# Two stacked 5x5 convolutions: earlier additions to v, another buffer for one v, and column filtering in seven more chunks

## The chip, the cores and the metric

The kernel runs on one core of a Trainium2 chip. The metric is the device time of one execution in microseconds (us), lower is better. Five engines take their instructions in order from queues of their own: TensorE (PE: matrix products), VectorE (DVE: elementwise work), ScalarE (ACT: copies, scalings, activations with sums), GpSimd (POOL: small copies, and the issue of those DMAs that add to what is there) and SyncE (SP: the issue of other DMAs). They wait for one another by semaphores.

## The reference

The input x is 8 images of 32 channels, 252 x 252, in float32. Two layers of the same form follow each other:

```
def _gn(v, G=16, eps=1e-5):        # mean and variance over 2 channels and the image
    ...
    return ((g - m) / jnp.sqrt(s + eps)).reshape(v.shape)
x = x + _L0_conv_ref(_gn(x), L0_conv_weight)
x = x + _L1_conv_ref(_gn(x), L1_conv_weight)
```

`_L0_conv_ref` and `_L1_conv_ref` are 5 x 5 convolutions from 32 to 32 channels with reflected borders (written with FFTs). A layer can only begin on an image when that image's mean and variance are known; for the second layer these are those of the first layer's output.

## The kernel before

**Tiling.** The pixels of an image are put on the 128 partitions as 32 channels times 4 parities (even or odd row, even or odd column). A 5 x 5 filter becomes a 3 x 3 one on this grid. In the direction of rows the kernel uses a minimal filter with six points, numbered 0 to 5: from groups of rows it forms six combinations, multiplies each with transformed weights on TensorE, and puts four output rows together from the six products. An image of a layer is cut into 8 chunks; a chunk (b, l, c) is image b, layer l (0 or 1), chunk c. So there are 128 chunks. In a chunk each point takes three matrix products (one for each column of the filter) of 504 columns (layer 0) or 508 (layer 1). The trace shows each product as two records.

**Before the products**, in `transform`: `v` holds differences or sums of rows. In layer 0 VectorE forms it (`row_pairs`, L561). In layer 1 it is made by DMAs from GpSimd's queue (`row_sums`): L551 copies the chunk's rows of `y` (the first layer's output) into a `v` tile, and once the copy has landed L553 and L554 add further rows. Then VectorE forms from `v` and from the rows the operands: `point2` (L586), `point4` (L590), `point1` (L596), `point3` (L593), and for points 0 and 5 `points05` (L603). L590, L593 and L603 read `v`; L603 is its last reader.

**The v tiles.** There are two, with tags `va` and `v`, of one buffer each. Layer 0 uses `v`. Layer 1 uses `va`; only from chunk 6 of the last but one image on do layer-1 chunks take `va` and `v` in turn.

**Column filtering** (`by_columns`): in some chunks points 0 and 5 are not computed with 2 x 3 full products (group `sums`, written by L679), but with 8 products of half the width (L701), after a filter in the direction of columns as well. This asks for four more operations on VectorE ahead (`columns`: L612, L613 and L621, L622, or L616 in their place in layer 0), three behind (`column_parts`: L786, L787, L788) and one on ScalarE between the products (`seed_columns`: L705, which scales one PSUM bank into another). In layer 1 chunks 1, 3 and 5 do so, in the last image but one only 1 and 3.

**After the products**, in `conv`: ScalarE seeds the PSUM banks of points 1 and 3 (L723, L725) from those of points 2 and 4, and copies these to the tile `sd` (L731, L738). VectorE combines them (L742, L751, L752, L757, L758), ScalarE or VectorE writes the outer rows (L767, L779, L765), and in layer 1 ScalarE interleaves the output rows to `o` (L916), which SyncE stores. The products of points 0 and 5 of most chunks come one chunk late, behind the `m` and `pairs` products (points 2, 4 and 1, 3) of the next chunk.

**Statistics** (`finish_stats`): six small steps on VectorE, TensorE and ScalarE turn sums into mean and scale: `moments` (ends with L336), `group_mean` (TensorE, L342 and L344), `deviations` (begins with L351), `group_var` (L363), `variance` (L369, L371), `inverse` (L377 to L383). ScalarE scales the weights with the result (`scale_points`, L511, three pairs of points) and GpSimd adds the residual's own weights (`add_residual`, L479, four operations for each pair). For the last chunk of layer 0 of each image these steps run twice: for the next image's layer 0, and for this image's layer 1.

**Order.** All is put into one table with due times (`at`), sorted, and issued in that order (`manual_schedule`); on each engine the instructions keep it. A due time is thus only a place in a queue. `begin(i)` gives the planned start of the i-th chunk; it is shorter for chunks that filter by columns. Layer 0 of image b + 1 and layer 1 of image b take turns, chunk by chunk; two pairs are swapped, so that the sequence at the start of layer 1 is (1,0,0), (1,0,1), (0,1,0), (0,1,1), (1,0,2).

Of the kernel before, what the change touches and what calls it, by code (L numbers as in the profile page):

```python
# [56 lines left out]
def tile_conv_preact_x2(ctx: ExitStack, tc: tile.TileContext, x: bass.AP, w0: bass.AP, w1: bass.AP, out: bass.AP):  # L57
    nc = tc.nc
    B, C, H, W = x.shape
# [5 lines left out]
    NCH = 8  # L65
# [26 lines left out]
    def at(t: float, fn, *args, **kw):  # L92
        table.append((t, len(table), fn, args, kw))
# [67 lines left out]
    def once(b: int, c: int) -> bool:  # L161

        return c < (NCH - 1, 3)[b] if b < 2 else False

    def parts(b: int, c: int):

        if once(b, c):
            return ((0, 10), (10, 6)) if (b, c) == (0, 0) else ((0, 2), (2, 14))
        return ((0, ROWS),) + (((ROWS, 2),) if c == NCH - 1 else ())
# [216 lines left out]
    def finish_stats(b: int, l: int, *times):  # L386
        for t, fn in zip(times, (moments, group_mean, deviations, group_var, variance, inverse)):
            at(t, fn, b, l)
# [86 lines left out]
    def add_residual(eng, u, ks):  # L475
        for cp, rp in quads:
            to = (2 * (1 - cp) + (1 - rp)) * Q
            dst = u[quad(cp, rp), ks, 1 + cp, to : to + Q]
            eng.tensor_add(dst, dst, resid[quad(cp, rp), ks])  # L479
# [53 lines left out]
    def transform(t0: float, t1: float, b: int, l: int, c: int, free: float = -100.0, now=(0, 0, 0)):  # L533
# [4 lines left out]
        def source():  # L538
            if l == 0:
                nxt = xs[b, c + 1] if c + 1 < NCH else xtail[b]  # L540
                return xs[b, c][:, :, 0:256:2], nxt[:, :, 0:256:2]
            return ytile[b, c], ytile[b, c + 1] if c + 1 < NCH else ytail[b]

        def row_sums(add: bool):

            t, nxt = source()
            if not add:
                i = max(order.index((b, l, c)) - order.index((B - 2, 1, NCH - 2)), 0)
                got["v"] = vpool.tile([P, ROWS, wi], F32, tag=("va", "v")[i % 2], name=f"v_{b}_{l}_{c}")
                got["vt"] = got["v"].rearrange("p (t i) w -> p t i w", i=4)  # L550
                G.dma_start(got["v"], t)  # L551
            else:
                G.dma_start(got["v"][:, 0 : ROWS - 2], t[:, 2:ROWS], accum_op=ALU.add)  # L553
                G.dma_start(got["v"][:, ROWS - 2 : ROWS], nxt[:, 0:2], accum_op=ALU.add)  # L554
# [70 lines left out]
        if (b, l, c) == order[0]:  # L625
            at(t0 - 33.3, row_quads, 0, 2)
            at(t0 - 31, point2, 0, 2)
            for fn in (row_pairs, point4):
                at(t0, fn, 0, 2)
            at(t0 + 0.2, row_quads, 2, 4)  # L630
            at(t0 + 0.2, row_pairs, 2, 4)
            at(t0 + 0.2, last_rows)
            at(t0 + 0.2, point2, 2, 4)
            at(t0 + 0.2, point4, 2, 4)
            at(t0 + 4.9, point1)
            at(t0 + 5.5, point3)
            at(t0 + 6.2, points05)
        else:
            if l:
                two = begin(order.index((b, l, c)) - 2)  # L640
                at(two + 1.45, row_sums, False)
                at(two + 11.0, row_sums, True)
            else:
                at(t0, row_pairs)
            for dt, fn in ((2, row_quads), (3.2, last_rows), (3.6, point2)):
                at(t0 + dt, fn)
            at(max(t0 + 4.2, free + 9.45) if l else t0 + 4.2, point4)
            at(max(t0 + 5.5, free + 7.8), point1)
            at(max(t0 + 5.6, free + (11.1 if by_columns(*now) else 10.25)), point3)
            at(t1, points05)  # L650
            if by_columns(b, l, c):
                at(t1 + 1.5, columns)
# [292 lines left out]
    order = [(0, 0, c) for c in range(NCH)]  # L945
# [4 lines left out]
    for n in ((0, 1, 0), (B - 2, 1, NCH - 2)):  # L950
        i = order.index(n)
# [8 lines left out]
    def by_columns(b: int, l: int, c: int) -> bool:  # L960
        if l == 0:
            return c < NCH - 1 and (b > 1 or (b == 1 and c > 1))
        return c in ((1, 3, 5) if b == B - 1 else ((1, 3) if b == B - 2 else (1, 3, 5)))

    own = [5.1 if i in at_once else 1.7 if by_columns(*n) else 0.0 for i, n in enumerate(order)]
    late = [0.0 if i in at_once else 1.7 if by_columns(*n) else 5.1 for i, n in enumerate(order)]
# [1 line left out]
    def begin(i: int) -> float:  # L968

        return sum(10.2 + (own + [0.0])[j] + (late[j - 1] if j else 0.0) for j in range(i))  # L970


    t0 = -100.0
# [37 lines left out]
    at(t0 + 32.5, variance, 0, 0)  # L1011
    at(t0 + 33.5, inverse, 0, 0)
    transform(t0 + 64, 0.0, *order[0])
    at(t0 + 19, residual_blocks)
    at(t0 + 63.7, first_point, 2)
# [11 lines left out]
    for i, (b, l, c) in enumerate(order):  # L1027
        t0, t1, t2 = (begin(i + j) for j in range(3))
        if i in at_once:
            conv(b, l, c, t0, t1, m05=(extra[:, 0], extra[:, 1]))  # L1030
        elif i + 1 == len(order):

            conv(b, l, c, t0, t0 + 12.75, 0.0, 0, 2, m05=(extra[:, 0], extra[:, 1]))
            conv(b, l, c, t0 + 12.75, t0 + 20.4, 0.0, 2, 4, m05=(sums05[:, 0], sums05[:, 1]))
        elif i + 2 == len(order):
            conv(b, l, c, t0, t1, t1 + 10.3, later=5.1)
        else:
            conv(b, l, c, t0, t1, t2, later=10.2 + own[i + 1])
        if i + 1 < len(order):
            transform(t0 + (6.3 if i == 0 else 2.9), t1 + 0.2, *order[i + 1], free=t0, now=(b, l, c))  # L1040
            nb, nl, ncx = order[i + 1]
            k = inputs.index((nb, ncx)) + 2
            if nl == 0 and 2 < k < len(inputs):
                for part in parts(*inputs[k]):
                    early = once(*inputs[k]) or nb == 0
                    at(t0 + (14.0 if nb == 0 and part[0] == ROWS else 4.0 if early else 9.5), load, *inputs[k], *part)
                    at(t1 + (0.2 if early else 9.0), borders, *inputs[k], *part)
                    if once(*inputs[k]):
                        kb, kc = inputs[k]
                        t = 5.25 if part[0] == 0 and (kb, kc) != (1, 0) else 13.55 if kb else 8.5  # L1050
                        at(t1 + t, even_columns, *inputs[k], *part)
        if c == 0 and any(by_columns(b, l, k) for k in range(NCH)):
            t = begin(i - 1) if l == 0 and b > 1 else t2 if l == 0 else t0
            at(t + 5.4, halve_middle, b, l)
            at(t + 8.2, column_weights, b, l)
        if b and l == 0 and c == 0:
            at(t0 + 0.1, begin_sums, b, 1)

        if l == 0 and b + 1 < B:
            wide = 1 if b == 0 else 2  # L1060
            if c == 0:
                for j in range(2):
                    at(begin(i - 1) + 1.0 if b > 1 else t0 + (8.0 if b else 1.0), load_piece, b + 1, j)
            if c < NPIECE // 2:
                for j in range(2):
                    p = 2 * c + j
                    t = (t1 if wide == 2 and j else t0) + (8.6 + 2.5 * j if wide == 1 else 9.8)
                    if b == 1 and p < 4:
                        t = begin(NCH + (1, 1, 2, 2)[p]) + (9.8, 12.4, 9.8, 15.5)[p]
                    at(t, piece_sums, b + 1, p)  # L1070
                    if p + 2 < NPIECE:
                        at(t + 2.6, load_piece, b + 1, p + 2)
            if c == 2:
                at(t0 + 14, fetch_weights, b + 1, 0)
            if c == NCH - 1:
                finish_stats(b + 1, 0, *(t0 + t for t in (1.55, 3.5, 3.6, 6.9 if b else 7.7, 7.8, 8.4)))
                for j, ks in enumerate(pairs):
                    at(t0 + (9.5, 10.4, 11.3)[j], scale_points, b + 1, 0, ks)
                    at(t0 + (10.4, 12.3, 14)[j], lambda b=b, ks=ks: add_residual(G, scaled[b + 1, 0], ks))
        if l == 0 and c == NCH - 1:  # L1080
            te = t0 + 15.3
            at(te + 0.1, fetch_weights, b, 1)
            finish_stats(b, 1, *(te + t for t in (3.0 if b < B - 1 else 4.4, 6.85, 6.86, 10.25 if b else 9.9, 12.82, 13.55)))
            for j, ks in enumerate(pairs):
                at(te + (14.5, 15.5, 21)[j], scale_points, b, 1, ks)
                at(te + (15.5, 17.5, 22)[j], lambda b=b, ks=ks: add_residual(G, scaled[b, 1], ks))
# [36 lines left out]
```

## Time and profile before

| | us |
|---|---|
| median of 3 runs (range) | 1921.32 (1920.58 to 1922.4) |
| the profiled execution, whole | 1922.81 |
| its span, first to last instruction | 1921.0 |
| an image in the middle (377.87 to 608.12 and the like) | 229.7 to 230.3 |
| ScalarE busy, share of the span | 73% |
| DMA engines, mean busy share over a middle image | 0.94 to 0.95 |
| granted TensorE clock, mean | 0.99 |

In the lines of the profile "A <- B" tells which tile is written from which; a bracket at the end of a line in a timeline is the time that the engine was idle ahead of that instruction and what ended it. In the tables of waits the figures are total us, number, longest. A line of the table by stretches has the stretch, its length, then busy time and count for each of PE, PEld, DVE, ACT and POOL, and at the end the granted clock, the DMA share and GB/s. Durations of neighbouring instructions overlap a little, so that their distance from start to start is the better price of one in a row.

### The profile page before, as it was taken

The page shows a single profiled execution, that of the slowest core. Times are in us where ns is not written, and L with a number is a line of the kernel's source. Part 1 is how long each engine was busy: PE and PEld are TensorE (multiplying, and loading weights), DVE is VectorE, ACT ScalarE, POOL GpSimd, SP SyncE. Part 2 cuts the span into 40 slices and gives each one's busy share as a digit, 9 for nine tenths or more (in the row PEclk, how much of TensorE's full clock was granted, in tenths as well). Part 3 has the DMA queues.
Part 4 walks back from the last instruction along what each step waited for, and adds up shares of the span by engine and source line. Part 5 has one row for each costly group of instructions (what it writes and reads, how often), then busy time and mean ns, then how long its engine had stood idle before and what let it go on. Part 6 is the DMA issues. An engine that isn't in the chain of part 4 may idle for free.

```text
span 1921.0 us, 19939 instructions
## 1 busy us (share of the span) xinstructions
PE 1864.5 (97%) x5134; PEld 954.9 (50%) x5134; DVE 1673.9 (87%) x2923; ACT 1394.6 (73%) x2688; POOL 385.1 (20%) x733
## 2 busy tenths in 40 slices
PE   5998899999999999999999999999999999999998
PEld 4443355545555455544555445554455545544445
DVE  7987699989998899989999899997999989988675
ACT  5887577777787787777887777886787766665575
POOL 4542211131111211122111311113111131111210
PEclk8999899999999999999999999999999999999999
DMA  9877689989999899999999989998999978985695
GB/s 276 206 167 206 147 233 218 238 216 225 245 227 221 212 262 223 223 234 208 248 230 218 230 216 249 225 224 217 215 259 212 236 168 183 202 190 149 168 229 112
DMA packets 248626, 411.40 MB, mean 214 GB/s; under 512 B 19520, under 2 KB 215488, under 8 KB 238144
## 3 DMA queue, kind: packets, MB, share of 16 engines
q1 hardware_dynamic: 220384, 272.09, 60.4%
q0 software_dynamic: 27648, 135.28, 28.0%
q10 hardware_dynamic: 480, 2.77, 0.4%
q8 instruction: 40, 0.66, 0.1%
q14 instruction: 74, 0.61, 0.1%
HBM read 207.41 MB, written 67.39 MB: 143 GB/s over the span
## 4 chain that ended last, share of the span: by engine, by line
PE 83%; DMA 5%; ACT 4%; DVE 4%; issue 2%; POOL 1%; SPq 0%; ACTq 0%; DVEq 0%; POOLq 0%
PE pairs L679 30%; PE m L679 28%; PE sums L679 9%; PE extra L701 6%; PE sums L701 6%; PE extra L679 4%; DMA v<-y 2%; DMA st<-in_x_dram 2%; ACT o L916 1%; POOL u L479 1%; ACT junk L854 1%; ACT st L231 0%; ACT y L777 0%; ACT sd L731 0%; DVE sd L742 0%
## 5 line engine op out<-in xcount | busy, mean ns | idle before, releaser
L679 PE MATMUL m<-t,u 128*128 128x508 f32 (+3 forms) x1560 | 682.0, 585 | 21.4 <-POOL u L479 12.8
L679 PE MATMUL pairs<-t,u 128*128 128x504 f32 (+2 forms) x1548 | 688.8, 584 | 4.2 <-ACT pairs L723 2.8
L679 PEld LDWEIGHTS m<-t,u 128*128 128x128 f32 x1560 | 294.3, 190 | 346.4 <-issue 299.5
L679 PEld LDWEIGHTS pairs<-t,u 128*128 128x128 f32 x1548 | 290.0, 189 | 329.9 <-issue 303.5
L916 ACT COPY o<-y 64x508 f32<-64x508 f32 x496 | 326.8, 659 | 8.7
L679 PE MATMUL sums<-t,u 128*128 128x508 f32 (+5 forms) x492 | 208.4, 572 | 0.0
L725 ACT COPY pairs<-m 128x504 f32<-128x504 f32 (+1 forms) x129 | 72.5, 562 | 151.1 <-PE m L679 123.2
L742 DVE SCALAR_TENSOR_TENSOR sd<-sd,pairs 128x504 f32<-128x504 f32 (+2 forms) x258 | 164.2, 670 | 18.4 <-PE pairs L679 15.2
L854 ACT ACTIVATE junk<-y,negk 128x1008 bf16<-128x1008 f32 (+1 forms) x144 | 147.3, 1023 | 25.2 <-PE extra L701 14.9
L603 DVE SCALAR_TENSOR_TENSOR t<-v 128x1024 f32<-128x1024 f32 (+1 forms) x128 | 157.2, 1228 | 9.5 <-PE sums L679 9.5
L731 ACT COPY sd<-m 128x504 f32<-128x504 f32 (+2 forms) x258 | 137.2, 584 | 18.6 <-DVE sums L788 12.5
L590 DVE SCALAR_TENSOR_TENSOR t<-v 128x512 f32<-128x512 f32 (+2 forms) x129 | 90.4, 701 | 65.7 <-DMA v<-y 52.0
L701 PE MATMUL extra<-sdiff,wc 128*128 128x252 f32 (+2 forms) x560 | 141.6, 374 | 0.6 <-ACT extra L705 0.4
L701 PEld LDWEIGHTS extra<-sdiff,wc 128*128 128x128 f32 x560 | 104.2, 188 | 74.6 <-issue 51.4
L679 PEld LDWEIGHTS sums<-t,u 128*128 128x128 f32 x492 | 91.7, 188 | 94.6 <-issue 88.2
L767 ACT ACTIVATE y<-sums 128x508 f32<-128x508 f32 (+2 forms) x80 | 42.5, 580 | 130.3 <-PE sums L679 130.3
L148 POOL COPY xs<-xs 64x32 f32<-64x32 f32 (+3 forms) x74 | 35.2, 476 | 488.3 <-DMA xs<-in_x_dram 378.4
L561 DVE TENSOR_TENSOR v<-xs 128x1792 f32<-128x1792 f32 (+1 forms) x65 | 130.2, 2003 | 1.8 <-issue 0.5
L701 PE MATMUL sums<-d,u 128*128 128x252 f32 (+2 forms) x560 | 130.5, 375 | 0.0
L237 ACT ACTIVATE st<-st,negk 128x1134 f32<-128x1134 f32 x98 | 121.7, 1242 | 3.2
L553 POOL DMA_DIRECT2D v<-y x64 | 55.3, 863 | 319.2 <-DMA v<-y 319.2
L701 PEld LDWEIGHTS sums<-d,u 128*128 128x128 f32 x560 | 105.0, 189 | 26.2 <-issue 12.8
(171 smaller groups left out, 2467.7 us busy)
## 6 DMA issues: line engine op xcount, KB each, us to landing
xs<-in_x_dram SPq DMA_DIRECT2D x176, 504.0 KB, 11.6
v<-y POOLq DMA_DIRECT2D x64, 1032.0 KB, 5.4
st<-in_x_dram SPq DMA_DIRECT2D x111, 567.0 KB, 6.9
out_dram<-o SPq DMA_DIRECT2D x488, 126.0 KB, 5.3
v<-y POOLq DMA_DIRECT2D x64, 903.0 KB, 10.5
u<-ud SPq DMA_DIRECT2D x15, 1152.0 KB, 5.6
xs<-in_x_dram SPq DMA_DIRECT2D x30, 441.0 KB, 6.5
xs<-in_x_dram SPq DMA_DIRECT2D x28, 472.5 KB, 10.8
```

The lines of the kernel that those rows point to most:

```text
L237: A.activation(junk, src, AF.Square, bias=negk, accum_out=acc[:, 1, i : i + 1])
L553: G.dma_start(got["v"][:, 0 : ROWS - 2], t[:, 2:ROWS], accum_op=ALU.add)
L561: V.tensor_sub(v[:, r0:r1], t[:, r0 + 2 : r1 + 2], t[:, r0:r1])
L590: stt(ts[b, l, c][0][:, 1, j0:j1], vt[:, :, 1], -2.0, vt[:, :, 2], ALU.mult, ALU.add)
L603: stt(t, got["vt"][:, :, 0:2], 4.0 if l else -4.0, got["vt"][:, :, 2:4], ALU.mult, ALU.add)
L679: T.matmul(dst, u[:, k, 2 - i, :], rhs[:, j0 + i0 : j0 + i1, i : i + wo], start=(i == 0 and not add), stop=(i == 2), skip_group_check=add,)
L701: T.matmul(dst[:, 0, use], w, rhs[:, use], start=(i == 2), stop=True, skip_group_check=(i != 2))
L725: A.copy(dst, src)
L731: A.copy(got["sd"][:, 1 + e], m24[e][:, 0:n])
L742: stt(d, d, -2.0, pairs13[e][:, 0:n], ALU.mult, ALU.add)
L854: A.activation(dst, src, AF.Square, bias=negk, scale=1.0 if i else -1.0, accum_out=acc[:, 1, at_ : at_ + 1])
L916: copy(got["o", h][halves[s], 0:m, cp::2], got["y"][halves[cp], r : r + m, :])
```

## The change

Four places are edited. (1) The v tile of chunk 1 of image 0 in layer 1 takes tag `v`. (2) The step that adds to v is due 8.4 rather than 11.0 after the planned start of the chunk two before. (3) In layer 1, column filtering is done in chunks 1, 3, 5 and 7 of images 0 to 5, in 1 and 3 of image 6 (as before), and in 1, 2, 4, 5 of image 7. (4) In the statistics of the next image's layer 0, `group_mean` and `deviations` are due 0.9 later. `begin`, which counts from `by_columns`, changes with (3).

```diff
             if not add:
-                i = max(order.index((b, l, c)) - order.index((B - 2, 1, NCH - 2)), 0)
+
+                i = max(order.index((b, l, c)) - order.index((B - 2, 1, NCH - 2)), 1 if (b, c) == (0, 1) else 0)
                 got["v"] = vpool.tile([P, ROWS, wi], F32, tag=("va", "v")[i % 2], name=f"v_{b}_{l}_{c}")
...
                 at(two + 1.45, row_sums, False)
-                at(two + 11.0, row_sums, True)
+                at(two + 8.4, row_sums, True)
...
     def by_columns(b: int, l: int, c: int) -> bool:
         if l == 0:
             return c < NCH - 1 and (b > 1 or (b == 1 and c > 1))
-        return c in ((1, 3, 5) if b == B - 1 else ((1, 3) if b == B - 2 else (1, 3, 5)))
+        return c in {B - 1: (1, 2, 4, 5), B - 2: (1, 3)}.get(b, (1, 3, 5, 7))
...
-                finish_stats(b + 1, 0, *(t0 + t for t in (1.55, 3.5, 3.6, 6.9 if b else 7.7, 7.8, 8.4)))
+                finish_stats(b + 1, 0, *(t0 + t for t in (1.55, 4.4, 4.5, 6.9 if b else 7.7, 7.8, 8.4)))
```

In the resulting instruction streams, at each of the six later image changes GpSimd's L553 and L554 stand ahead of the first four L479 instead of behind them, and L222 behind these. At the start of layer 1, L553 and L554 of chunk (0,1,1) stand ahead of the border copies (L148, L153, L154) instead of behind. In the last image they stand ahead of the last four L479. On ScalarE, at the six image changes, the third L511 stands ahead of L725 instead of behind L731, one L705 is new ahead of the first L511, and the next chunk's L705 stands behind the border copies (L863 to L866, L861) instead of ahead. SyncE's stream is unchanged.

## Prediction

> **What bounds the kernel now.** I read the page's first part, then the waits of TensorE, then timelines around the waits.
>
> ```profile
> PE 1864.5 (97%) x5134; PEld 954.9 (50%) x5134; DVE 1673.9 (87%) x2923; ACT 1394.6 (73%) x2688; POOL 385.1 (20%) x733
> ...
> PE m L679 <- POOL u L479: 12.8, 1, 12.8
> PE m L342 <- DVE mv L332: 4.8, 6, 0.8
> PE m L679 <- ACT o L916: 2.9, 5, 0.8
> PE pairs L679 <- ACT pairs L723: 2.8, 7, 0.5
> ```
>
> TensorE is the bound: 97% busy, and past the head its waits come to some 30 us. So just two things shorten the run: fewer matmul columns, or removing one of these waits. The others count only where TensorE ends up waiting for them. The largest wait is one place, where layer 2 starts (timelines of GpSimd, VectorE and TensorE):
>
> ```profile
> 176.77 1.21 POOL L554 DMA_DIRECT2D v<-y  x1
> 195.87 0.55 POOL L551 DMA_DIRECT2D v<-y  x1 [17.89 <-DVE t L603]
> 196.43 3.84 POOL L479 TENSOR_TENSOR u<-u,resid 32x64 f32<-32x64 f32 x8
> ...
> 190.73 0.70 DVE L590 SCALAR_TENSOR_TENSOR t<-v 128x516 f32<-128x516 f32 x1 [11.64 <-DMA v<-y]
> ...
> 198.81 8.39 PE L679 MATMUL m<-t,u 128*128 128x508 f32 x12 [12.85 <-POOL u L479]
> ```
>
> GpSimd wants to issue the copy of the second layer-2 chunk, (0,1,1), into `va`. The first chunk, (0,1,0), still holds it until VectorE's L603 (ends 195.5), which stands behind L590, which waits for the sums DMA. The residual additions to the weights queue behind that copy, and the first layer-2 matmul behind them. Twelve matmul records take 5.11 elsewhere, 8.39 here; the stretches 198.8 to 202 and 202 to 205 say why:
>
> ```profile
> 198.80:202.00 3.20, 3.19 (x4) 1.50 (x5) 0.00 (x0) 0.00 (x0) 2.86 (x9) 0.50 0.29 111
> 202.00:205.00 3.00, 3.00 (x5) 1.10 (x4) 0.00 (x0) 0.66 (x1) 1.92 (x5) 0.52 0.98 193
> ```
>
> The third figure from the right is the granted clock: half. The gap costs 12.85 + 3.3 us.
>
> The other place is the image change, alike six times (here the second):
>
> ```profile
> 622.87 1.23 DVE L603 SCALAR_TENSOR_TENSOR t<-v 128x1032 f32<-128x1032 f32 x1
> 627.43 0.16 DVE L351 COPY mean<-m 128x1 f32<-128x1 f32 x1 [3.34 <-PE m L342]
> 651.09 0.70 DVE L590 SCALAR_TENSOR_TENSOR t<-v 128x516 f32<-128x516 f32 x1 [3.26 <-DMA v<-y]
> ...
> 624.40 0.60 POOL L551 DMA_DIRECT2D v<-y  x1 [2.52 <-DVE t L603]
> 637.33 2.23 POOL L479 TENSOR_TENSOR u<-u,resid 32x64 f32<-32x64 f32 x4 [12.13 <-ACT u L511]
> 639.50 0.88 POOL L553 DMA_DIRECT2D v<-y  x1
> ...
> 646.86 4.64 PE L679 MATMUL sums<-t,u 128*128 128x508 f32 x12
> 663.49 5.31 PE L679 MATMUL m<-t,u 128*128 128x504 f32 x12 [0.26 <-ACT o L916]
> ```
>
> VectorE is idle 3.34 us before the mean and 3.26 before L590; GpSimd issues v's sums only after the residual additions.
>
> **The change part by part.** Times are read in the profiled execution.
>
> *A. The other v buffer, once.* Chunk (0,1,1) takes tag `v`, whose last reader is L603 of layer-1 chunk (1,0,1), ended at 173.7. So its copy is issued right behind L554, at 178.0, and the eight residual additions run from 178.7, in 3.8 us as now or as far as ScalarE's L511 (178.2, 180.5) allows: weights of points 2 and 4 are ready at 180.8. TensorE finishes its work at 185.96 and goes on: point 2 (six records, 2.55) to 188.5, point 4 when L590 has run (190.73 + 0.69 = 191.4), to 194.0. Now it is 207.2: 13.2 us won. Late next: point 3 waits for VectorE's L757 and its seed (0.2 us), and points 0 and 5 for the last four additions, which stand on GpSimd behind the moved L553 and L554 and so behind the landing of the early copy. SyncE's queue keeps its order. The first `va` is then free for (0,1,2) as well, so that copy goes out earlier too, after these.
>
> Here a rule speaks against the edit. The row: at 180 to 190 the DMA engines are at a share of 1.10 with 238 GB/s, so no gap takes 1.03 MB more. The Trainium skill (DMA: Bandwidth & Descriptors, "Issuing engines are not separate DMA queues") says all queues run on the same 16 engines and interleave. If the copy takes its whole time from the sums already under way, 1.03/0.238 = 4.3 us, L590 moves to 195.0 and point 4 to 195.7, a gap of 7.2 us, which may bring the half clock (another 3.3): 7.0 us won less the stalls, 6. If it goes behind them, since both are issued to the same queue, L590 stays. I take the second; but the copy itself then lands at about 195.8 (the DMA engines are through at 191.5 now, plus 4.3), L553 and L554 end at 197.8, the borders at 198.5, four additions (1.5) at 200.0, and points 0 and 5 wait 0.7 us at 199.3. **A: 13.2 - 0.2 - 0.7 = 12.3; ends 6 and 13.2.**
>
> On the clock: TensorE: Matmul & The Clock Gate ("What's actually happening") puts the drop to half after an idle window of about 3.4 us. The trace has a gap of 1.36 at 178.7 with no mark and one of 12.85 with the full mark; 2.9 us lies between, so by the rule nothing is added, by the nearer row nothing either. At 7.2 us the rule adds up to 3.3.
>
> *B. group_mean a product later* (3.5 to 4.4; deviations with it). The instruction streams show L342 behind a sixth `m` product instead of the fifth. Six times TensorE waited about 0.8 for L332 there; a product is two records, 5.11/6 = 0.85. It covers the wait; the mean comes 0.05 later. **6 x 0.75 = 4.5; ends 4.0 and 4.8.** At the first image, where nothing waited, it costs VectorE 0.1 us, hidden.
>
> *C. Columns in chunk 7 of six images.* Removed: 12 records of `sums`, 4.48 (to 651.34). Added: 16 of 256, 252, 192 and 189 columns; eight such in mixed width take 1.49 to 1.51 by the first chunks' L701 rows. So 1.46 saved, 8.8 in six. VectorE gets four operations at L612 to L622 of 0.60 each, 2.4 us, placed between L603 and L351: inside the 3.34 us of idle time. And three at L786 to L788, 1.95 with their waits, behind L758, where nothing is idle; the 3.26 after it pays for that, if v comes earlier (D). ScalarE gets L705 (0.49) between two `o` copies and L511. TensorE's second column product waits for it: the copies end at 635.0 (shifted by B), L705 at 635.5, products ready at 635.2: 0.3 us. In the next chunk L705 now stands behind the border copies: 0.2. If ScalarE doesn't shift with B, 1.1 rather than 0.3. The next chunk's `sdiff` is ready at 644.6, needed at 644.7: just in time, and without that cover each us of VectorE shows. **C: 8.8 - 6 x 0.5 = 5.8; ends 1 and 8.8.**
>
> *D. v's sums ahead of the residual additions* (11.0 to 8.4). The streams show the pair L553, L554 before the first four additions at these six places, otherwise in place save for one border copy at A and one at the last image. GpSimd issues them when the copy has landed: 624.4 + 5 (4.5 to 7 elsewhere in the stage) = 629.5, before L511 frees the additions at 637.3, so these lose nothing. v lands at 641 with the old 11.4 us, ten earlier; at 647.8 (651.09 - 3.26), plus 1.95 of C, less 0.8 of B, L590 runs at 649.0 instead of 651.1: 2.1 earlier (2.1 to 2.7 over the six), where TensorE arrives 1.75 earlier (B and C). The waits at the next `m` (0.26 to 0.84, six times, 3.6 in all; named ScalarE, but L586 of VectorE ended 0.15 before it) come from this chain and go. The following 0.4 at L723 I leave. **D: 3.6; ends 0 and 5.5.**
>
> *E. Last image*, columns in 1, 2, 4, 5 for 1, 3, 5: one chunk from 18 x 0.852 = 15.33 to 13.64 (12 x 0.852 and eight short products, 3.42): **1.7; ends 0.5 and 1.7.** VectorE needs 13.0 us in such a chunk (8.65 and 4.35), under 13.6; today's idle there is 2 us and more.
>
> Sum: 12.3 + 4.5 + 5.8 + 3.6 + 1.7 = 27.9. The span of 1921.0 becomes 1893; the profiled execution, 1922.8, becomes 1894.9. The median shown, 1921.32, lies 1.5 below that execution: 1893.4.
>
> **The rivals.** *R1, the early copy collides* (above): A is 6, the sum 21.6: 1900. For it the share of 1.10; against it the common queue. *R2, the image change takes C and D back*: VectorE and ScalarE are close there (L705, `sdiff`), or the DMA engines, 0.95 busy over an image, deliver later: left are A, B, E, 18.5: 1903. Against it: the stretch at which the sums now go out, 1090 to 1094 in the fourth, has a DMA share of 0.58. *R3, the tag changes nothing*, because TensorE waits at layer 2's start for L590 anyway until near 198: A 0 to 3, so 1903 to 1906; against it, L590 runs at 190.7. *R4, slower*: GpSimd is in order, so the residual additions now stand behind the landing of v's copy, at each image change. They are needed by TensorE at 649.6, take 2.2, and L553 with L554 1.8: free while the copy takes under 21 us from 624.4, then one us each per image. To eat the 28 us it must take 26; at 27 us the loss is 6 x 6 = 36 and the time 1929. GpSimd's longest wait for such a copy was 9.4, though a more crowded DMA is what the change itself makes. *R5*: gains of the parts given back to DMA, within 0.2% (3.8 us).
>
> **How the numbers follow.** My forecast 0.70 (1887 to 1898), R1 0.10, R2 0.08, R3 0.04, R4 0.06, R5 0.02. Low end: all parts at their good ends, 13.2 + 4.8 + 8.8 + 5.5 + 1.7 = 34: 1887. High end: all at their bad ends, 6 + 4 + 1 + 0 + 0.5 = 11.5: 1909; it holds R1 to R3 and leaves R4 and R5, 0.08, outside. Faster by over 0.2% (what a measurement here tells from no change) 0.92, within 0.02, slower 0.06.
>
> **What would show it.** Right: no wait of TensorE for L479; point 2 at 186, a gap of about 3 before point 4, no half clock at 200; no wait for L332; L590 at image changes without a DMA wait; image to image 227.6 (less 0.75, 0.97 and 0.6) instead of 229.9; new short waits for L705. Wrong: a gap over 5 us at 188 (R1), `extra` waiting for VectorE (R2), `m` waiting for L479 at an image change (R4).

## The result, and the profile after

| | before | after |
|---|---|---|
| median, us (range, runs) | 1921.53 (1920.58 to 1922.4) | 1895.52 (1892.25 to 1899.39, 4) |
| ratio to before, 95% interval | | 0.9866, 0.9843 to 0.9888 |
| profiled execution, span | 1922.81, 1921.0 | 1893.14, 1891.4 |

The change makes the kernel 26 us faster by the medians; between the two spans of the profiled executions it is 29.6, of which 1.5 are the state of TensorE's clock in the last image and not the change (last section). "Layer 2" means the second layer, whose chunks have l = 1. An added blank line moves the code: from L548 on, the line numbers of after are one higher (L590 is now L591, L705 is L706, L679 is L680).

First the page's part on engines, then the waits of TensorE (total, times, longest), both of after:

```profile
PE 1851.5 (98%) x5162; PEld 956.7 (51%) x5162; DVE 1698.0 (90%) x2972; ACT 1401.1 (74%) x2695; POOL 372.9 (20%) x733
```

```profile
PE m L680 <- DVE t L591: 2.6, 2, 2.0
PE extra L702 <- ACT extra L706: 2.6, 9, 0.9
PE m L680 <- DVE var L369: 2.1, 1, 2.1
...
PE m L342 <- DVE mv L332: 1.1, 2, 0.9
```

TensorE is busy 13 us less and has far less to wait for: the 12.8 us for L479 are gone, the six waits of 0.8 for L332 are two with 1.1 in all, the waits for `o` no longer show. The second line has grown from two such waits (0.4 us in all) to nine, for the seed of the column products, and the first from one of 0.6 to two, one of them of about 2 us, for L591. The timelines of GpSimd, VectorE and TensorE at the start of layer 2 show why, in after:

```profile
176.79 1.22 POOL L552 DMA_DIRECT2D v<-y  x1
178.16 1.78 POOL L479 TENSOR_TENSOR u<-u,resid 32x64 f32<-32x64 f32 x4 [0.15 <-ACT u L511]
180.45 1.44 POOL L479 TENSOR_TENSOR u<-u,resid 32x64 f32<-32x64 f32 x4 [0.51 <-ACT u L511]
193.75 0.88 POOL L554 DMA_DIRECT2D v<-y  x1 [11.86 <-DMA v<-y]
...
189.62 0.70 DVE L591 SCALAR_TENSOR_TENSOR t<-v 128x516 f32<-128x516 f32 x1 [10.59 <-DMA v<-y]
...
185.69 2.72 PE L680 MATMUL m<-t,u 128*128 128x508 f32 x6
190.46 2.79 PE L680 MATMUL m<-t,u 128*128 128x508 f32 x6 [2.05 <-DVE t L591]
...
196.03 2.82 PE L680 MATMUL pairs<-t,u 128*128 128x508 f32 x6 [0.23 <-ACT pairs L726]
199.15 5.38 PE L680 MATMUL extra<-t,u 128*128 128x508 f32 x12 [0.29 <-POOL u L479]
204.50 1.94 PE L680 MATMUL sums<-t,u 128*128 128x504 f32 x4
```

The copy of the second chunk goes out at 176.79, the first eight residual additions run right behind it as far as ScalarE's L511 lets them, and point 2 starts at 185.69. What is left of the big gap is 2.05 us, the landing of the first chunk's sums (L591). The next `sums` group starts at 204.50; before it was 217.39, so 12.9 us come from here. The table by stretches (granted clock third from the right) shows no half clock behind the small gap:

```profile
190.00:194.00 4.00, 3.54 (x9) 1.68 (x10) 4.00 (x9) 1.80 (x6) 0.25 (x1) 1.00 0.96 369
194.00:198.00 4.00, 3.77 (x10) 1.53 (x9) 3.86 (x8) 1.86 (x4) 3.74 (x7) 1.00 0.77 158
```

The second image change of after, again by the timelines of the three engines:

```profile
608.71 0.60 POOL L552 DMA_DIRECT2D v<-y  x1
613.81 0.87 POOL L554 DMA_DIRECT2D v<-y  x1 [4.50 <-DMA v<-y]
620.74 2.23 POOL L479 TENSOR_TENSOR u<-u,resid 32x64 f32<-32x64 f32 x4 [5.16 <-ACT u L511]
...
610.86 0.14 DVE L351 COPY mean<-m 128x1 f32<-128x1 f32 x1
632.50 0.69 DVE L591 SCALAR_TENSOR_TENSOR t<-v 128x516 f32<-128x516 f32 x1
...
619.27 1.02 PE L702 MATMUL extra<-sdiff,wc 128*128 128x256 f32 x4 [0.22 <-ACT extra L706]
```

GpSimd issues the additions to v before the residual additions, which still wait for ScalarE and lose nothing. Both idle times of VectorE are gone (no bracket at L351, none at L591), and the seed costs TensorE a short wait.

Where the 29.6 us came from, by the starts of the second layer's statistics products on TensorE (L342 with `avg_yy`, one for each of the eight images; the second of them is at 396.86 before and 383.12 after):

| stretch | before | after | less |
|---|---|---|---|
| to the first late `sums` of layer 2 | 217.39 | 204.50 | 12.9 |
| from there to the second of these products | 179.47 | 178.62 | 0.85 |
| five images, to the seventh | 1149.83 | 1138.31 | 11.5 |
| to the eighth | 219.01 | 217.44 | 1.6 |
| from there to the end | 155.30 | 152.53 | 2.8 |

Over the five images one takes 227.66 on average instead of 229.97. But the five are not alike: 226.90, 228.27, 227.42, 228.85, 226.87. Before, all lay within 0.6 us. Below, an image change is called undisturbed where TensorE's waits in it are no longer than 0.25 us.

### The profile page after: what moved, and what is told of

Its sections match the earlier page's. It is cut to its first block, busy times and chain, and to the rows that moved or that the text cites. A ratio compares the mean times of both kernels' runs of the same rounds, so it can differ in the third digit from the quotient of the medians.

```text
span 1891.4 us, 20043 instructions
## 1 busy us (share of the span) xinstructions
PE 1851.5 (98%) x5162; PEld 956.7 (51%) x5162; DVE 1698.0 (90%) x2972; ACT 1401.1 (74%) x2695; POOL 372.9 (20%) x733
## 4 chain that ended last, share of the span: by engine, by line
PE 76%; DVE 9%; DMA 8%; ACT 3%; issue 2%; POOL 1%; SPq 0%; DVEq 0%; ACTq 0%; POOLq 0%
PE m L680 27%; PE pairs L680 26%; PE sums L680 8%; PE sums L702 6%; PE extra L702 6%; DMA v<-y 4%; PE extra L680 4%; DMA st<-in_x_dram 1%; DMA xs<-in_x_dram 1%; DMA out_dram<-o 1%; DVE sd L743 1%; ACT o L917 1%; DMA v<-ytail 1%; DVE t L604 1%; POOL u L479 0%
## 5 line engine op out<-in xcount | busy, mean ns | idle before, releaser
L680 PE MATMUL pairs<-t,u 128*128 128x504 f32 (+2 forms) x1548 | 690.4, 585 | 2.7 <-ACT pairs L726 1.6
L680 PE MATMUL m<-t,u 128*128 128x508 f32 (+3 forms) x1560 | 675.2, 581 | 7.1 <-DVE t L591 2.6
L680 PEld LDWEIGHTS m<-t,u 128*128 128x128 f32 x1560 | 293.3, 189 | 325.6 <-issue 297.4
L680 PEld LDWEIGHTS pairs<-t,u 128*128 128x128 f32 x1548 | 289.2, 189 | 321.5 <-issue 295.6
L680 PE MATMUL sums<-t,u 128*128 128x508 f32 (+5 forms) x408 | 175.3, 578 | 0.0
L702 PE MATMUL extra<-sdiff,wc 128*128 128x252 f32 (+3 forms) x616 | 156.3, 375 | 3.3 <-ACT extra L706 2.6
L702 PEld LDWEIGHTS extra<-sdiff,wc 128*128 128x128 f32 x616 | 113.5, 188 | 89.6 <-issue 50.2
L591 DVE SCALAR_TENSOR_TENSOR t<-v 128x512 f32<-128x512 f32 (+2 forms) x129 | 89.7, 695 | 65.6 <-DMA v<-y 47.7
L702 PE MATMUL sums<-d,u 128*128 128x252 f32 (+3 forms) x616 | 142.3, 373 | 0.0
L554 POOL DMA_DIRECT2D v<-y x64 | 55.2, 863 | 377.7 <-DMA v<-y 377.7
L702 PEld LDWEIGHTS sums<-d,u 128*128 128x128 f32 x616 | 115.3, 189 | 26.9 <-issue 11.8
L148 POOL COPY xs<-xs 64x32 f32<-64x32 f32 (+3 forms) x74 | 34.1, 461 | 450.2 <-DMA xs<-in_x_dram 330.7
L680 PEld LDWEIGHTS sums<-t,u 128*128 128x128 f32 x408 | 75.9, 188 | 80.1 <-issue 77.2
L231 ACT ACTIVATE st<-st 128x1134 f32<-128x1134 f32 x98 | 112.2, 1145 | 4.0 <-DMA st<-in_x_dram 2.8
```

The costliest lines, as they stand in the source:

```text
L231: A.activation(junk, src, AF.Identity, accum_out=acc[:, 0, i : i + 1])
L591: stt(ts[b, l, c][0][:, 1, j0:j1], vt[:, :, 1], -2.0, vt[:, :, 2], ALU.mult, ALU.add)
L680: T.matmul(dst, u[:, k, 2 - i, :], rhs[:, j0 + i0 : j0 + i1, i : i + wo], start=(i == 0 and not add), stop=(i == 2), skip_group_check=add,)
L702: T.matmul(dst[:, 0, use], w, rhs[:, use], start=(i == 2), stop=True, skip_group_check=(i != 2))
```

## The experiments

Each kernel is before, or the changed kernel, with the edit shown. "Image" is the mean of the five distances above, from the profiled execution.

| kernel | median, us (range) | ratio, 95% interval | image |
|---|---|---|---|
| tag alone | 1911.24 (1910.14 to 1912.39) | 0.9938, 0.9922 to 0.9955 | 230.09 |
| all but the tag | 1902.97 (1901.41 to 1905.31) | 0.9898, 0.9883 to 0.9913 | 227.80 |
| all but the early sums | 1905.20 (1905.04 to 1906.13) | 0.9910, 0.9895 to 0.9924 | 229.58 |
| all but chunk 7 | 1894.45 (1893.01 to 1897.16) | 0.9854, 0.9839 to 0.9870 | 227.72 |
| mean alone | 1915.11 (1913.09 to 1916.09) | 0.9965, 0.9952 to 0.9977 | 229.07 |
| early sums alone | 1911.24 (1910.29 to 1911.73) | 0.9946, 0.9931 to 0.9961 | 228.48 |
| chunk 7 alone | 1922.27 (1919.65 to 1924.64) | 1.0002, 0.9993 to 1.0011 | 230.32 |
| last image alone | 1919.81 (1917.59 to 1922.72) | 0.9991, 0.9982 to 1.0001 | 229.97 |
| changed, first v early | 1887.78 (1886.56 to 1892.98) | 0.9828, 0.9815 to 0.9842 | 227.15 |
| and the last image further | 1886.34 (1885.41 to 1891.72) | 0.9821, 0.9808 to 0.9835 | 227.07 |
| and chunk 7 not filtered | 1889.55 (1889.08 to 1890.78) | 0.9833, 0.9820 to 0.9847 | 227.88 |
| changed, seed earlier | 1899.49 (1895.23 to 1902.80) | 0.9883, 0.9869 to 0.9896 | 228.37 |

The kernel before stood at 1922.24 beside the first four, at 1921.8 beside the next four and at 1921.9 beside the last four.

**The tag, alone and left out.**

```diff
-                i = max(order.index((b, l, c)) - order.index((B - 2, 1, NCH - 2)), 0)
+                i = max(order.index((b, l, c)) - order.index((B - 2, 1, NCH - 2)), 1 if (b, c) == (0, 1) else 0)
```

> Only the other v buffer for chunk (0,1,1), all else as before. Theory (the sum of parts): the two traces put 12.9 us of the gain here, so 1908.6 against 1921.5, with no wait of TensorE for L479 and a gap of 2 us ahead of point 4. Rival (the early copy's load comes back): later DMAs are late by what was won, and less than 6 us are left: 1915 or more. On the spread of the changed kernel (7 us where the kernel before has 2): if it comes from the clock of TensorE in the gap at the start of layer 2, it shows here too; if from VectorE's just-in-time work at the image changes, this kernel stays within 2 us.

> The whole change but for the v buffer. Theory: 12.9 us worse than the changed kernel, 1908; the gap of 12.85 us and the half clock are back. Rival (parts are not independent, the change needs the tag): over 1912. Spread: as wide as in the changed kernel if VectorE at the image changes makes it, within 2 us if the gap at the start of layer 2 does.

Alone it brings 11.0 us, where 12.9 were expected. In its profile the gap before point 4 was 3.50 us, against 2.05 in after, 1.43 in the kernel without chunk 7 and 2.31 in that without the early sums; the clock stayed full behind all four. A fifth kernel with the tag, the last one below, whose edit leaves this place as it is, had a gap of 3.16 and the half clock behind it (its timeline of TensorE):

```profile
191.83 5.42 PE L680 MATMUL m<-t,u 128*128 128x508 f32 x6 [3.16 <-DVE t L591]
```

Six records took 5.42 us there and 2.79 in after. So the late `sums` of layer 2 began between 203.58 and 207.71 in these five profiles: the tag was worth 9.7 to 13.8 against the 217.39 of before. Left out, it costs 7.5 against the changed kernel's median, less than the 12.9 expected. The profile of that kernel has the gap again (12.38), but the half clock behind it ended earlier (its twelve records took 6.77, before 8.39); its late `sums` began at 215.00, 10.5 after those of the changed kernel.

With the tag in, TensorE waited at this place for L591 (L590 in kernels without the blank line) and no longer for the residual additions. Nor was that step delayed by 4 us, as a collision would do: it ran at 189.24 to 191.78 in these five profiles, and at 189.28 to 191.26 in the six without the tag, that of before included. R1 and the empty tag, R3, are out.

**All but the early sums; all but chunk 7.**

```diff
-                at(two + 8.4, row_sums, True)
+                at(two + 11.0, row_sums, True)
```

```diff
-        return c in {B - 1: (1, 2, 4, 5), B - 2: (1, 3)}.get(b, (1, 3, 5, 7))
+        return c in {B - 1: (1, 2, 4, 5), B - 2: (1, 3)}.get(b, (1, 3, 5))
```

> The whole change, but v's sums due at 11.0 as before, so behind the first four residual additions. Theory (the early sums are the cover of the new column chunk): L590 at the image changes waits for its DMA again, VectorE comes 0.8 us earlier than before where TensorE comes 1.75 earlier; the waits at the next m return (3.6) and grow by 0.95 in each of six: 9 us worse, about 1904. Rival (VectorE's idle time pays for the column chunk by itself, and the early sums bring only their own 3.6): 1899. Rival (they bring nothing): 1896.

> The whole change, but chunk 7 of images 0 to 5 without column filtering. Theory: 5.8 us worse than the changed kernel (8.8 of TensorE less 3.0 of new stalls): 1901. Rival (VectorE takes the column chunk's gain back): same as the changed kernel within 2 us, 1896. Spread: within 2 us if VectorE's load at the image changes makes it, as wide as in the changed kernel if the gap at the start of layer 2 does.

Without the early sums 9.7 us are lost, as expected (9). Without chunk 7 nothing is lost: 1894.45 against 1895.52, where my sum had 5.8 for it. So the early sums carry more than I gave them, and the column filtering in chunk 7 less.

**The parts alone: mean, early sums, chunk 7, last image.** The edits are those of the change, each by itself.

> Only group_mean and deviations later (4.4, 4.5). Theory: six waits of 0.8 us less 0.05 each go, 4.5 us: 1917, and no wait of TensorE for L332. Rival (the mean is late for what follows, or VectorE is the bound behind it): within 1 us of the kernel before, the time showing up as waits at the next m or pairs.

> Only v's sums ahead of the residual additions (8.4). Theory: VectorE no longer waits 3.3 to 3.8 us at L590, the waits at the next m (3.6 in all) and at L723 (2.0) go: 3.6 to 5.6 us, 1916 to 1918. Rival (the residual additions are delayed behind the copy's landing): not faster than before, with waits of m for L479.

> Only column filtering in chunk 7 of images 0 to 5. Theory: without the early sums VectorE's three new operations fall inside its wait for v, but it comes no earlier, so TensorE gains 8.8, loses 3.0 at L705, and waits 1 us more at the next m of each image: 0 to 1 us, 1920 to 1921. Rival (the parts are independent): 5.8 us, 1916.

> Only the last image's chunks 1, 2, 4, 5 for 1, 3, 5. Theory: 15.33 - 13.64 = 1.7 us: 1919.8, with no new wait of TensorE after 1780. Rival (two such chunks in a row are more than VectorE can do): 1921 or slower, with waits for L614 or L706.

The mean brings 6.7. The last image brings 2.0, with an interval that just includes no change. The early sums bring 10.6, three times my 3.6; chunk 7 brings nothing. The timelines of VectorE and TensorE with the early sums alone, behind the second image change:

```profile
645.24 0.69 DVE L590 SCALAR_TENSOR_TENSOR t<-v 128x516 f32<-128x516 f32 x1
...
659.22 1.67 PE L701 MATMUL sums<-d,u 128*128 128x189 f32 x8
660.72 5.23 PE L679 MATMUL m<-t,u 128*128 128x504 f32 x12
665.79 3.54 PE L679 MATMUL pairs<-t,u 128*128 128x504 f32 x8
```

L590 no longer waits, and both waits behind it are gone: the one at `m` (0.26 in this image) and the one at L723 (0.40), which I had left standing. They also cost more than their brackets say. The `sums` group is busy 1.67 us, but undisturbed the next group starts 1.50 behind its start, since neighbours overlap. Before, the distance was 661.56 to 663.49, 1.93: 0.43 lost for a bracket of 0.26. At the `pairs` it was 5.71 against 5.07 now: 0.64 for a bracket of 0.40. The bracket begins at the end of the group ahead, an end that the profile models; the overlap is lost in addition, 0.17 to 0.24 a wait. It was alike for the mean: 0.90 an image (229.97 to 229.07) for flagged 0.8.

The timelines of VectorE and TensorE with chunk 7 alone, at the same place:

```profile
649.97 0.69 DVE L590 SCALAR_TENSOR_TENSOR t<-v 128x516 f32<-128x516 f32 x1 [1.87 <-DMA v<-y]
...
635.04 1.02 PE L701 MATMUL extra<-sdiff,wc 128*128 128x256 f32 x4 [0.22 <-ACT extra L705]
...
649.21 5.27 PE L679 MATMUL m<-t,u 128*128 128x508 f32 x12
...
662.36 5.31 PE L679 MATMUL m<-t,u 128*128 128x504 f32 x12 [1.26 <-ACT o L916]
```

From the statistics product (625.79) to `m` at 649.21 it is 23.42, before 24.23: 0.81 of the 1.46 us saved are left behind the wait for the seed. Then the wait at the next `m` has grown from 0.26 to 1.26. VectorE's added work is not the cause: VectorE still stands 1.87 us for v before L590. But v comes no earlier (L590 runs 24.18 after the statistics product, before 23.98), so what TensorE gained ahead of it is lost in the wait behind it. The early sums are thus the cover of chunk 7. In the profiles they bring 1.92 an image with chunk 7 filtered (229.58 without them, 227.66 with) and 1.49 alone.

**What is left of chunk 7 in the changed kernel.** In its two undisturbed images (226.87 and 226.90) it is 0.7 better than without chunk 7 (227.6). The other three lost 3.9 us together against these two. About half of that is at the image change with the longest waits, as timelines of VectorE, ScalarE and TensorE show:

```profile
1056.24 0.69 DVE L591 SCALAR_TENSOR_TENSOR t<-v 128x516 f32<-128x516 f32 x1 [3.01 <-DMA v<-ytail]
...
1068.08 0.15 DVE L351 COPY mean<-m 128x1 f32<-128x1 f32 x1
...
1068.27 0.66 ACT L724 ACTIVATE pairs<-m,means 128x508 f32<-128x508 f32 x1 [2.44 <-DVE mean L351]
...
1075.58 0.59 ACT L706 ACTIVATE extra<-extra 128x512 f32<-128x512 f32 x1
...
1068.98 1.12 PE L680 MATMUL pairs<-t,u 128*128 128x508 f32 x2 [0.33 <-ACT pairs L724]
...
1076.22 1.02 PE L702 MATMUL extra<-sdiff,wc 128*128 128x256 f32 x4 [0.88 <-ACT extra L706]
```

Chunk 7's own v landed late and VectorE stood 3.01 us. Before, an idle time of 3.34 ahead of L351 could take that up. Now the four column operations fill it, so L351 is late, ScalarE behind it, and the seed: TensorE waits 0.33 and 0.88. Other profiles bear this out. Where chunk 7 is not filtered, such a wait of VectorE of 2.11 left 1.21 idle ahead of L351 and TensorE no wait (in the kernel that is all but chunk 7). Where it is filtered, one of 1.95 (first v early) came with 0.44 at the seed instead of 0.21, and one of 3.27 (all but the tag) with 0.45 and 0.88.

The other half is at the waits for the mean of the next image's layer 0 (L332; 0.88 and 0.26 in two images). They stand ahead of chunk 7's column operations, so the filtering at that image change cannot be their cause; what made VectorE late there was not tried.

**The first v early; a further chunk of the last image; chunk 7 taken out again.**

```diff
-                at(two + 1.45, row_sums, False)
-                at(two + 8.4, row_sums, True)
+                first = (b, c) == (0, 0)
+                at(two + (-14.0 if first else 1.45), row_sums, False)
+                at(two + (-6.0 if first else 8.4), row_sums, True)
```

```diff
-        return c in {B - 1: (1, 2, 4, 5), B - 2: (1, 3)}.get(b, (1, 3, 5, 7))
+        return c in {B - 1: (1, 2, 3, 4, 5), B - 2: (1, 3)}.get(b, (1, 3, 5, 7))
```

The third kernel has both, and (1, 3, 5) for images 0 to 5.

> The changed kernel with the copy and the sums of v for the first layer-2 chunk, (0,1,0), issued some 15 us earlier, when the DMA engines are at a share of 0.14. Theory: the gap left at the start of layer 2 (2.05 us before point 4 in the changed kernel, 1.43 to 3.50 in the experiments so far) is the landing of those sums, and that landing is what differs from run to run: the gap goes, the short wait for the residual additions too, so 2 to 2.5 us less than the changed kernel (1893.0 to 1893.5 where that gives 1895.5). Rival: the gap is something else on VectorE, or the early copy takes DMA time from the weights of layer 2: no gain, 1895 to 1896, or a later first product.

> As the run before it, and in the last image columns in chunk 3 too (1, 2, 3, 4, 5). Theory: one more chunk whose 18 records of 0.852 become 12 and eight short ones, 1.7 us less, since VectorE needs 13.0 us of the 13.6 that TensorE then takes: 1.7 under the run before. Rival: five such chunks in a row leave VectorE no time to catch up, and TensorE waits for its differences: same as the run before, or slower.

> As the run before it, without the column filtering in chunk 7. Theory (the filtered chunk 7 brings nothing, as its saving of 1.46 us per image goes in waits for ScalarE's seed and in the cover of late v): the same as the run before within 2 us, with less spread between its runs (4 us or less, against 7 for the changed kernel). Rival (the step of 5.8 us is there and something else hid it): 4 to 6 us slower than the run before.

Timelines of GpSimd and TensorE with the first v early:

```profile
143.75 0.78 POOL L552 DMA_DIRECT2D v<-y  x1
149.06 0.88 POOL L554 DMA_DIRECT2D v<-y  x1 [4.54 <-DMA v<-y]
...
186.32 5.27 PE L681 MATMUL m<-t,u 128*128 128x508 f32 x12
192.62 5.35 PE L681 MATMUL pairs<-t,u 128*128 128x508 f32 x12 [1.04 <-ACT pairs L725]
```

The twelve records of points 2 and 4 run in one piece; a wait of 1.04 for the seed of point 1 is next. Up to the first image that is 1.44 us (363.54 against 364.98 at the first layer's statistics product, L342 with `avg_ss`). The median fell by 7.7, far more than expected. Some of the rest stands in the images of its profile (227.15 on average against 227.66). Why they are less disturbed when v of the first chunk is early was not tried, and stays open. One candidate for another part is that this kernel has no gap before point 4 and so no half clock behind it, which the changed kernel may have in runs without a trace (the gap of 3.16 above shows that the place can); that is not shown. The range of its runs is still 6.4 us wide, against 7.1 for the changed kernel. So the landing of the first v does not alone spread the changed kernel's runs, and that half of my theory falls. Of the others the tag alone spread 2.3 us, all but the tag 3.9, all but chunk 7 4.2 and all but the early sums 1.1. But the kernel before, too, spread 1.8 to 6.9 over its four sets of runs, so what spreads them stays open.

The last image's fifth filtered chunk gives the lowest median of the study, 1886.34. Its step, 1.4 by the medians with intervals that overlap, agrees with the 1.7 expected (the last image takes 150.75 instead of 152.53 in after, both at full clock). Taking chunk 7 out again costs 3.2 by the medians, with intervals that overlap, and 0.81 an image in the profiles (227.07 to 227.88), 4.9 in six; the range shrinks from 6.3 to 1.7, as expected. So "chunk 7 brings nothing", which I expected here, is wrong as a rule: it brings 0.7 to 0.8 an image where the image change is undisturbed, and the changed kernel loses as much in its disturbed ones.

**The seed one place earlier in chunk 7.**

```diff
-            at(t0 + 9.3, seed_columns)
+            at(t0 + (8.15 if l and c == NCH - 1 else 9.3), seed_columns)
```

> The changed kernel with one edit: in the filtered chunk 7 the halving of extra (L706) stands ahead of ScalarE's last two o copies, 1.3 us earlier; every other engine's stream is as in the changed kernel. Theory: the second column product waited for it (flagged 0.21 in undisturbed images, more in others), so this wait goes from every image change, 0.3 to 0.5 us each: 2 to 3 us less than the changed kernel, 1892.5 to 1893.5, an undisturbed image 226.4 to 226.6 instead of 226.9. Rival (what C lost is the cover of late v alone): same as the changed kernel, and the lost time stays at the waits for the mean and the pairs.

The edit does more than I meant: at 8.15 the halving also comes ahead of the first column product (8.5) in the recorded order, so in chunk 7 it halves what the bank held before, the middle columns get wrong values, and the first product waits for the halving. The timeline of TensorE:

```profile
622.31 1.02 PE L702 MATMUL extra<-sdiff,wc 128*128 128x256 f32 x4 [1.33 <-ACT extra L706]
...
624.88 0.92 PE L702 MATMUL extra<-sdiff,wc 128*128 128x256 f32 x4
```

A wait of 1.33 stands at the first product and the one of 0.22 at the second is gone; an image without further waits takes 227.93 to 228.04 instead of 226.87 to 226.90. That is 1.1 us for 1.1 us more of waiting: TensorE's time in such an image follows the seed's place directly. The 4.0 us by the medians (6.6 between the profiled spans) are not the seed's alone: 3.2 of the 6.6 had been lost before the late `sums` of layer 2 began, by the gap of 3.16 and the half clock behind it. Whether a seed between its product and the last `o` copies would gain was not settled by it.

## Why the prediction came out as it did

The time, 1893.4 forecast and 1895.52 measured, lies in the range named for it (1887 to 1898), and the profiled execution, 1893.14, is near the 1894.9 of the sum. But that the sum holds is luck: two errors, in C and in D, cancel.

- **A, 12.3: right.** 12.9 in place: point 2 at 185.69 (predicted 186), a gap of 2.05 (about 2.9), no half clock, 0.23 for the seed of point 3 (0.2), 0.29 for the residual additions (0.7). Of the two readings of the shared DMA engines the second held, that the copy goes behind the sums: L591 ran at 189.62, not later than the 190.73 of before, and over eleven profiles the tag did not shift it. That the common queue is the reason was not tried by itself. That the clock stayed full is in part luck: the same place lost 2.6 us to the half clock in another profile, behind a gap of 3.16, where the forecast added nothing at 2.9. (In the same part the 7.0 for a collision does not follow from its figures: point 4 from 195.7 to 198.3 leaves 8.9 of the 207.2, or 5.6 with the half clock.)
- **B, 4.5: right step, a little too small.** 6.7 alone by the medians, 0.90 an image by the profiles, where 0.75 was forecast. I priced the wait at its bracket; the overlap of neighbours is lost on top. Six times 0.90 is 5.4; where the rest of the 6.7 comes from is open.
- **C, 5.8: failed.** The step that fell is "2.4 us, placed between L603 and L351: inside the 3.34 us of idle time". That idle time was cover for a v that lands late; filled, a landing that holds VectorE some 2 us or more goes on through the mean and the seed to TensorE. The waits for the seed are as predicted where nothing else is late (0.22 flagged for 0.3, up to 0.2 at the next chunk). Alone C gave 0.0, as v then comes no earlier. Taking it out of the changed kernel lost nothing, where an undisturbed image gained 0.7 to 0.8 of the 0.97 forecast; the disturbed images lost as much, about half of it by this chain and half by the waits for L332. R2 had this mechanism, for C alone: D was not taken back.
- **D, 3.6: mechanism right, size wrong.** v's sums go out at 613.81, the additions lose nothing (so not R4), L591 has no wait. The term for the waits at the next `m`, 3.6 in all, was mis-sized, and "The following 0.4 at L723 I leave" was wrong: it came from the same late chain. Alone 10.6; by the profiles 1.49 an image, of which the flagged waits are 0.6 and 0.4 and two overlaps 0.4. I had seen that D was what paid for C, and still priced D by the waits that exist without C.
- **E, 1.7: right.** 2.0 alone by the medians, not clear of noise; the last image with E alone took 152.23 against 153.99 with the early sums alone, both at full clock: 1.76.

The parts alone add up to 11.0 + 6.7 + 10.6 - 0.5 + 2.0 = 29.8 by the medians. The whole is 26.0 by the medians, so up to 3.8 got lost between the parts; which of them lost it the runs do not show, and the spread of the changed kernel's runs (7.1) is wider than that. Of the signs named ahead, the wait for L332 came back twice (0.88 and 0.26, in disturbed images), and the mean image, 227.66, hit the 227.6 by the same cancelling.

## What to carry to other kernels

A wait of the bounding engine is worth its bracket and the overlap with the instruction ahead of it, some 0.2 us here: compare distances from start to start with and without the wait, and add up all waits that come from one late chain. Idle time of another engine ahead of a step that the bound waits for is not free room when a DMA lands just before it with some spread: it is the cover of the late landings. And time saved on the bounding engine ahead of a landing that does not move is lost again in the wait for it. Price parts that cover for one another as a pair, and test each alone and each left out.

## What the hardware showed that was not expected

In the last image TensorE has one gap of 2.08 us, for the variance (L369), the same in all 14 traces. Behind it the granted clock fell to half in five of them and stayed full in nine. The tables by stretches for the same place, before first, then after (granted clock third from the right):

```profile
1775.30:1778.30 3.00, 3.00 (x5) 1.19 (x4) 2.31 (x9) 1.80 (x3) 0.71 (x2) 0.50 0.91 344
```

```profile
1748.50:1751.50 3.00, 2.99 (x8) 1.22 (x7) 2.54 (x10) 1.83 (x3) 0.71 (x2) 1.00 0.90 350
```

Eight records take 5.37 at half clock and 3.67 at full, and the next group starts 1.5 us later. The other four were the tag alone, all but the early sums, all but chunk 7, and the first v early, so it doesn't follow the edit. So 1.5 of the 2.8 us of the last stretch in the table are no part of the change. At layer 2's start the gap of 3.16 had the half clock behind it; those of 1.43, 2.05, 2.31 and 3.50 did not. So the 3.4 us of idle time that the Trainium skill gives for the drop (TensorE: Matmul & The Clock Gate, "What's actually happening") is not the bound for a single gap here: 2.08 was enough five times in fourteen, 3.16 was in its one case, and 3.50 was not in its one case. What decides between them the runs do not show.
